# A feed-forward's second product as seven block products in place of eight, with its layer norm on another engine

## The chip, the cores and the metric

The kernel runs on one core of a Trainium2 chip. A core has five engines that run at the same time and wait for each other through semaphores: TensorE (PE in the profile; its weight loads, PEld, overlap with its matmuls), VectorE (DVE), ScalarE (ACT), GpSimd (POOL) and SyncE (SP), which here only issues DMA transfers. SBUF is the on-chip memory, PSUM the accumulator memory that TensorE writes. The metric is the device time of one execution in microseconds (us).

## The reference

A block over 4096 tokens of width 256, all in float32. `xn` is the normalized input; the output is the input plus an attention branch and a mixture of eight experts, both fed with `xn`.

```
xn   = layernorm(x)                                   # 4096 x 256
x1   = xn + attention(xn)                             # 8 heads, windows of 64
x2   = (x1 - mean) * rsqrt(var + eps) * gamma + beta  # second layer norm
h    = gelu(x2 @ W1 + b1)                             # 4096 x 1024
ffn  = x2 + h @ W2 + b2                               # second product: 1024 -> 256
moe  = sum over each token's two best experts of share * expert(xn)
out  = x + ffn + moe
```

## The kernel before

The order of the instructions on every engine is written out by hand: what the source says first comes first in that engine's queue. The work has three parts. A first stage (to about 50 us) normalizes the input, chooses experts and sorts tokens by expert. A long stage (to about 859 us) runs attention and the experts side by side; an expert's unit covers one or two tiles of 128 tokens, and its results go to the table `done` in device memory, the attention's to `x1d`. The last units (`whole`, lines 919 and 1301 to 1309) run only where the counts ask for them; those of one tile use matmuls with 128 moving columns (line 832). While this stage ends, at lines 1218 to 1235, the pools of attention are closed, `W1`, `W2` and the vectors are loaded, and the first group of the last stage is loaded and normalized.

The last stage is the feed-forward, from 859 us to the end: eight groups of 512 tokens (`NG`, four tiles `TG` of 128 tokens each). For a group `g`:

- `second_loads` (line 1070) loads `x2` from `x1d` and `acc` from the input, through SyncE's queue.
- `second_norm` (line 1077) normalizes: four `tensor_scalar` and the product with gamma on VectorE, then beta, `b2` and the sum into `acc` on GpSimd.
- `turned2` (line 1094) transposes `x2` on TensorE into `pt`, and VectorE copies it to `x2T`.
- `hidden` (line 1105) makes the eight chunks `ph` of 128x512 with two matmuls each; ScalarE writes gelu of them to `hT` (tile `hf`).
- `picked` (line 1120) gathers two rows of `done` per token with indirect DMAs that GpSimd issues, into eight buffers `got`; `combined` (line 1135) adds them to `acc` with their shares on VectorE.
- `second` (line 1143) makes the second product `pd`, 32 matmuls of 128x128 weights (`hT`) against 256 columns of `W2`, and VectorE adds it to `acc`; `store` writes `acc` out.

PSUM has seven banks that `bank` hands out in turn; a bank is written again only when its reader is done. In the loop TensorE's order is hidden(g), turned2(g+1), second(g-1), so the second product runs one group behind:

```
        if g > 0:
            acc = x2s.pop(g - 1)[0]
            list(second(g - 1, acc, before))
            combined(g - 1, acc, ys)
            store(g - 1, 0, TG, acc)
        before = hT
        ys = picked(g)
```

Of the kernel before, what the change touches and what calls it, by code (L numbers as in the profile page):

```python
# [32 lines left out]
F32 = mybir.dt.float32  # L33
# [68 lines left out]
def block_kernel(ctx: ExitStack, tc: tile.TileContext, a: dict, out: bass.AP):  # L102
# [11 lines left out]
    small = pool(ctx, "small", bufs=3)  # L114
    wexp = pool(ctx, "wexp", bufs=2)
    dram = ctx.enter_context(tc.tile_pool(name="dram", bufs=1, space=bass.MemoryType.DRAM))
# [12 lines left out]
    def halves(pb):  # L129
        return pb.rearrange("p (t n) -> p t n", t=2)  # L130
# [659 lines left out]

    he = pool(ctx, "he", bufs=2)
    sp = pool(att, "sp", right, bufs=2)
# [283 lines left out]

    def second_norm(g, acc, x2):

        for t in range(TG):
            i = g * TG + t  # L1080
            nc.vector.tensor_scalar(
                x2[:, t, :],
                x2[:, t, :],
                mv2[:, i, 0:1],
                r2[:, i : i + 1],
                ALU.subtract,
                ALU.mult,
            )
        nc.vector.tensor_tensor(x2, x2, bcast(gamma, TG, 1), ALU.mult)  # L1089
        nc.gpsimd.tensor_tensor(x2, x2, bcast(beta, TG, 1), ALU.add)  # L1090
        nc.gpsimd.tensor_tensor(acc, acc, bcast(b2, TG, 1), ALU.add)
        nc.gpsimd.tensor_tensor(acc, acc, x2, ALU.add)

    def turned2(g, x2):
        x2T = hf.tile([P, DC, G], F32, tag="x2T", name=f"x2T{g}")
        for c in range(DC):
            pt = bank(f"pt2_{g}_{c}")
            for t in range(TG):
                nc.tensor.transpose(  # L1099
                    pt[:, t * P : (t + 1) * P], x2[:, t, c * P : (c + 1) * P], ident  # L1100
                )
            nc.vector.tensor_copy(x2T[:, c, :], pt)  # L1102
        return x2T

    def hidden(g, x2T):
        hT = hf.tile([P, FC1, G], F32, tag="hf", name=f"hf{g}")
        for f in range(FC1):
            ph = bank(f"ph{g}_{f}")
            for c in range(DC):
                nc.tensor.matmul(  # L1110
                    ph,
                    W1[:, c, f * P : (f + 1) * P],
                    x2T[:, c, :],
                    start=(c == 0),
                    stop=(c == DC - 1),
                )
            nc.scalar.activation(hT[:, f, :], ph, AF.Gelu, bias=b1[:, f : f + 1])  # L1117
        return hT

    def picked(g):  # L1120
# [21 lines left out]

    def second(g, acc, hT):
        for t in range(0, TG, 2):
            pd = halves(bank(f"pd{g}_{t}"))
            for u in range(2):
                for f in range(FC1):
                    nc.tensor.matmul(  # L1148
                        pd[:, u, :],
                        hT[:, f, (t + u) * P : (t + u + 1) * P],  # L1150
                        W2[:, f, :],
                        start=(f == 0),
                        stop=(f == FC1 - 1),
                    )
            nc.vector.tensor_tensor(acc[:, t : t + 2, :], pd, acc[:, t : t + 2, :], ALU.add)  # L1155
            yield t

# [12 lines left out]
    STEPS = NT  # L1170
    flags = {}

    def load_unit(b):
# [5 lines left out]
    for b in range(ALWAYS):  # L1179
# [38 lines left out]
        if b == STEPS:  # L1218
            att.close()
            wf = pool(ctx, "wf", right)  # L1220
            hf = pool(ctx, "hf", right, bufs=2)
            accp = pool(ctx, "accp", right, bufs=4)
            got = pool(ctx, "got", right, bufs=8)
# [4 lines left out]
            late = pool(ctx, "late", right)  # L1228
            other.update({n: late for n in range(ALWAYS, BLOCKS, 3)})
            load_unit(ALWAYS)  # L1230
            for n in range(ALWAYS, BLOCKS):
                xs[n] = gather(n)
        if b == STEPS + 1:
            *_, r2 = rstd_of(mv2, root_of(mv2, NT, "b"), NT, "b")
            x2s[0] = second_loads(0)
        if 0 < b < STEPS:
# [55 lines left out]

    second_norm(0, *x2s[0])

# [123 lines left out]
```

## Time and profile before

| what | value |
|---|---|
| time, median of 3 runs | 1093.62 us (1093.41 to 1093.94) |
| profiled execution, its own time | 1094.16 us |
| its span in the profile | 1092.4 us |
| TensorE busy | 1079.8 us, 99% |
| VectorE, ScalarE, GpSimd busy | 598.3, 500.7, 503.3 us |
| granted TensorE clock | 1.00 throughout |
| last stage, TensorE's first transpose to the end | 858.8 to 1092.4 us |

The span is what the profiler saw on the core; the execution's own time has 1.76 us around it. A group of instructions is shown with its source line, engine, operation, the tile written and the tiles read, shapes and count; then busy time in us and the mean of one in ns; then idle time of the engine just before it and what ended that. The chain is the run of work that ended last, followed back from the end: start, duration, engine, tile, line, count. A float32 matmul leaves two records on TensorE (a transpose leaves one).

### The profile page before, as it was taken

What the parts mean: (1) busy time and instruction counts of PE and PEld (TensorE: products, weight loads), DVE (VectorE), ACT (ScalarE), POOL (GpSimd) and SP (SyncE); (2) the same over time, 40 slices, a digit from 0 to 9 for tenths busy, and PEclk for the clock granted to TensorE, in tenths of its full rate; (3) what the DMA queues carried; (4) which work ended last, traced back from release to release, by engine and by line L of the source; (5) the groups of instructions that cost most, each with busy time, mean ns of one, the idle gap of its engine ahead of it and who ended that gap; (6) DMA issues with size and microseconds to landing.
All of it is one profiled execution on the core that took longest, in us unless ns stands there. A gap on an engine that the chain in (4) does not pass through costs nothing. (4 is left out here: it accounts for less than half of the span.)

```text
span 1092.4 us, 18151 instructions
## 1 busy us (share of the span) xinstructions
PE 1079.8 (99%) x6424; PEld 855.0 (78%) x6424; DVE 598.3 (55%) x1633; ACT 500.7 (46%) x1170; POOL 503.3 (46%) x620
## 2 busy tenths in 40 slices
PE   8999999999999999999999999999999999999998
PEld 6577887887887888888888888888888666666667
DVE  6655766667666666676666666666542233332213
ACT  4526456645555556556645564566243322222220
POOL 5425543455346444653554455535123275555422
PEclk9999999999999999999999999999999999999999
DMA  9152445445355354454544544544386323333112
GB/s 293 62 232 78 141 148 175 172 140 176 134 167 178 127 182 161 159 181 148 194 140 158 168 177 141 197 149 177 134 311 221 104 77 97 96 97 97 58 58 77
DMA packets 60748, 163.37 MB, mean 150 GB/s; under 512 B 6288, under 2 KB 46608, under 8 KB 51184
## 3 DMA queue, kind: packets, MB, share of 16 engines
q1 hardware_dynamic: 54176, 144.48, 37.9%
q0 software_dynamic: 6480, 17.70, 5.8%
q8 instruction: 52, 0.85, 0.3%
q14 instruction: 40, 0.33, 0.1%
HBM read 140.28 MB, written 21.89 MB: 148 GB/s over the span
## 5 line engine op out<-in xcount | busy, mean ns | idle before, releaser
L832 PE MATMUL gu<-xsT,wg 128*128 128x256 f32 (+1 forms) x1632 | 362.5, 369 | 0.7 <-ACT xsT L824 0.7
L832 PEld LDWEIGHTS gu<-xsT,wg 128*128 128x128 f32 x1632 | 289.1, 190 | 45.3 <-DVE nm L961 8.6
L840 ACT ACTIVATE gs<-gu,wg 128x256 f32<-128x256 f32 (+1 forms) x204 | 93.0, 456 | 255.3 <-PE gu L832 249.3
L988 POOL TENSOR_TENSOR pr<-pr 128x256 f32<-128x256 f32 x128 | 93.1, 727 | 249.9 <-ACT pr L976 249.9
L841 DVE SCALAR_TENSOR_TENSOR hT<-gu,wg,gs 128x256 f32<-128x256 f32 (+1 forms) x204 | 95.2, 468 | 176.6 <-ACT gs L840 172.8
L894 PE MATMUL pe<-wd,hT 128*128 128x256 f32 x768 | 171.6, 379 | 0.0
L894 PEld LDWEIGHTS pe<-wd,hT 128*128 128x128 f32 x768 | 145.4, 190 | 20.5 <-issue 1.0
L989 POOL TENSOR_TENSOR pr<-pr,ident 128x256 f32<-128x256 f32 x128 | 126.3, 987 | 10.0
L976 ACT ACTIVATE pr<-pr,nm 128x256 f32<-128x256 f32 x256 | 127.4, 501 | 0.4
L1117 ACT ACTIVATE hf<-ph,b 128x512 f32<-128x512 f32 x64 | 44.1, 689 | 158.1 <-PE ph L1110 152.0
L1110 PE MATMUL ph<-x2T,W 128*128 128x512 f32 x256 | 111.3, 593 | 0.9 <-DVE x2T L1102 0.9
L1148 PE MATMUL pd<-W,hf 128*128 128x256 f32 x512 | 111.7, 379 | 0.0
L1148 PEld LDWEIGHTS pd<-W,hf 128*128 128x128 f32 x512 | 96.8, 190 | 13.3 <-issue 0.5
L961 DVE CUSTOM_DVE_ANT_0 pr<-ps,mask 128x256 f32<-128x256 f32 x256 | 90.7, 421 | 24.3 <-PE ps L947 24.3
L806 POOL DMA_INDIRECT xs<-xnd,token x71 | 68.9, 971 | 70.7 <-DVE paired_tiles L773 31.0
L1126 POOL DMA_INDIRECT got<-done,slot x64 | 63.4, 991 | 73.9 <-DVE acc L1139 60.9
L873 ACT ACTIVATE hT<-hT 128x512 f32<-128x512 f32 (+3 forms) x148 | 81.1, 548 | 32.0 <-DVE hT L841 21.8
L1110 PEld LDWEIGHTS ph<-x2T,W 128*128 128x128 f32 x256 | 48.5, 190 | 59.0 <-issue 57.6
L1090 POOL TENSOR_TENSOR x<-x,beta 128x1024 f32<-128x1024 f32 x8 | 18.8, 2349 | 88.4 <-DVE x L1089 88.4
L1155 DVE TENSOR_TENSOR acc<-pd,acc 128x512 f32<-128x512 f32 x16 | 11.0, 691 | 83.3 <-PE pd L1148 83.3
L1008 DVE TENSOR_TENSOR pr<-pr,rec 128x1024 f32<-128x1024 f32 x32 | 39.2, 1226 | 27.3 <-POOL pr L988 27.3
L976 ACT ACT_TABLE_LOAD x31 | 39.8, 1283 | 23.3 <-DVE nm L961 23.2
(213 smaller groups left out, 1440.5 us busy)
## 6 DMA issues: line engine op xcount, KB each, us to landing
wg<-in_gate_up SPq DMA_DIRECT2D x37, 1670.5 KB
wd<-in_down SPq DMA_DIRECT2D x37, 1024.0 KB
done<-y SPq DMA_DIRECT2D x30, 256.0 KB
x<-in_x SPq DMA_DIRECT2D x8, 512.0 KB
xnd<-xn SPq DMA_DIRECT2D x8, 512.0 KB
res<-xnd SPq DMA_DIRECT2D x16, 256.0 KB
x1d<-res SPq DMA_DIRECT2D x16, 256.0 KB
x<-x1d SPq DMA_DIRECT2D x8, 512.0 KB
```

What stands on the lines that cost most here:

```text
L806: nc.gpsimd.indirect_dma_start(out=x[:, t, :], out_offset=None, in_=xnd, in_offset=bass.IndirectOffsetOnAxis(ap=token[:, i : i + 1], axis=0),)
L832: nc.tensor.matmul(pb[:, k, :], w[:, lo : lo + P], xT[:, c, :], start=(c == 0), stop=(c == DC - 1),)
L840: nc.scalar.activation(gs, pb[:, 0, :], AF.Identity, bias=w[:, gb : gb + 1])
L841: nc.vector.scalar_tensor_tensor(hT[:, f, :], pb[:, 1, :], w[:, ub : ub + 1], gs, ALU.add, ALU.mult)
L873: nc.scalar.activation(hT[on, lo:hi, :], hT[on, lo:hi, :], AF.Silu)
L894: nc.tensor.matmul(pd, hT[:, f, t * P : (t + 1) * P], w[:, f * D : (f + 1) * D], start=False, stop=(f == FCM - 1),)
L961: nc.vector.tensor_tensor_reduce(out=pr[:, hh, j, :], in0=ps[hh][:, j, :], in1=mask[:, kind + j, :], scale=-1.0, scalar=-LOWEST, op0=ALU.a ...
L976: nc.scalar.activation(pr[:, hh, j, :], pr[:, hh, j, :], AF.Exp, bias=nm[:, j, hh : hh + 1], scale=-1.0, accum_out=sums[:, j, hh : hh + 1],)
L988: nc.gpsimd.tensor_tensor(first, first, second, ALU.add)
L989: nc.gpsimd.tensor_tensor(second, second, bcast(ident, 2, 1), ALU.mult)
L1110: nc.tensor.matmul(ph, W1[:, c, f * P : (f + 1) * P], x2T[:, c, :], start=(c == 0), stop=(c == DC - 1),)
L1148: nc.tensor.matmul(pd[:, u, :], hT[:, f, (t + u) * P : (t + u + 1) * P], W2[:, f, :], start=(f == 0), stop=(f == FC1 - 1),)
```

## The change

The second product of a group, (512 x 1024) times (1024 x 256), is seen as two by two blocks: tokens 0 to 255 and 256 to 511, hidden units 0 to 511 and 512 to 1023, output columns 0 to 127 and 128 to 255. Eight block products would make it; a scheme of Strassen's kind (Winograd's form) makes it with seven, from sums of blocks. The four sums of blocks of `W2` (tile `V2`) are made once on GpSimd, the four of a group's hidden activations (tile `hv`) on VectorE for each group, and the seven results are added to the four blocks of the output on VectorE, some by way of a tile `u`.

With it: the normalization goes to ScalarE as one activation per tile with scale and shift; gamma and beta are applied by the activation that takes the transposes out of PSUM, now on ScalarE too; `second_base` adds beta + b2 and gamma times the normalized rows to `acc` on VectorE; GpSimd keeps the gathers. In the loop, `second_loads` of group g+2 stands ahead of hidden(g), and `combined(g-1)` ahead of second(g-1). The pools of the experts close before the last stage, and its tiles `x2T`, `hf`, `hv`, `u` and `got` are placed where the experts' were.

```diff
-    def second_norm(g, acc, x2):
+    def second_norm(g, x2):
...
-            nc.vector.tensor_scalar(
+            nc.scalar.activation(
                 x2[:, t, :],
                 x2[:, t, :],
-                mv2[:, i, 0:1],
-                r2[:, i : i + 1],
-                ALU.subtract,
-                ALU.mult,
-            )
-        nc.vector.tensor_tensor(x2, x2, bcast(gamma, TG, 1), ALU.mult)
-        nc.gpsimd.tensor_tensor(x2, x2, bcast(beta, TG, 1), ALU.add)
-        nc.gpsimd.tensor_tensor(acc, acc, bcast(b2, TG, 1), ALU.add)
-        nc.gpsimd.tensor_tensor(acc, acc, x2, ALU.add)
+                AF.Identity,
+                bias=shift2[:, i : i + 1],
+                scale=r2[:, i : i + 1],
+            )
+
+    def second_base(g, acc, x2):
+
+        scaled = accp.tile([P, TG, D], F32, tag="scaled", name=f"scaled{g}", bufs=1)
+        nc.vector.tensor_tensor(acc, acc, bcast(beta_b2, TG, 1), ALU.add)
+        nc.vector.tensor_tensor(scaled, x2, bcast(gamma, TG, 1), ALU.mult)
+        nc.vector.tensor_tensor(acc, acc, scaled, ALU.add)
...
-            nc.vector.tensor_copy(x2T[:, c, :], pt)
+            nc.scalar.activation(
+                x2T[:, c, :], pt, AF.Identity, bias=beta_c[:, c : c + 1], scale=gamma_c[:, c : c + 1]
+            )
...
+    FH = FC1 // 2
+    F_LO, F_HI = slice(0, FH), slice(FH, FC1)
+    C1, C2 = slice(0, P), slice(P, D)
+
+    def sums_of_weights():
+        b11, b12, b21, b22 = W2[:, F_LO, C1], W2[:, F_LO, C2], W2[:, F_HI, C1], W2[:, F_HI, C2]
+        t1, t2, t3, t4 = (V2[:, k] for k in range(4))
+        for out_, left_, right_ in ((t1, b12, b11), (t2, b22, t1), (t3, b22, b12), (t4, b21, t2)):
+            nc.gpsimd.tensor_tensor(out_, left_, right_, ALU.subtract)
+
+    def sums_of_hidden(g, hT):
+        v = hf.tile([P, 4, FH, B], F32, tag="hv", name=f"hv{g}")
+        a11, a12, a21, a22 = hT[:, F_LO, 0:B], hT[:, F_HI, 0:B], hT[:, F_LO, B:], hT[:, F_HI, B:]
+        s1, s2, s3, s4 = (v[:, k] for k in range(4))
+        nc.vector.tensor_tensor(s1, a21, a22, ALU.add)
+        nc.vector.tensor_tensor(s2, s1, a11, ALU.subtract)
+        yield v
+        nc.vector.tensor_tensor(s3, a11, a21, ALU.subtract)
+        nc.vector.tensor_tensor(s4, a12, s2, ALU.subtract)
+        yield
+        return v
...
-    def second(g, acc, hT):
-        for t in range(0, TG, 2):
-            pd = halves(bank(f"pd{g}_{t}"))
...
-            nc.vector.tensor_tensor(acc[:, t : t + 2, :], pd, acc[:, t : t + 2, :], ALU.add)
+    def second(g, acc, hT, v):
+
+        t1, t2 = slice(0, 2), slice(2, 4)
+        u = hf.tile([P, 2, P], F32, tag="u", name=f"u{g}")
+
+        def product(n, left, right):
+            pb = bank(f"s{g}_{n}").rearrange("p (t n) -> p t n", n=P)[:, 0:2]
+            for t in range(2):
+                for f in range(FH):
+                    nc.tensor.matmul(
+                        pb[:, t, :],
+                        left[:, f, t * P : (t + 1) * P],
+                        right[:, f, :],
...
+        def add(t, cols, pb):
+            nc.vector.tensor_tensor(acc[:, t, cols], pb, acc[:, t, cols], ALU.add)
+
+        p1 = product(1, hT[:, F_LO, 0:B], W2[:, F_LO, C1])
+        nc.scalar.copy(u, p1)
+        add(t1, C1, u)
+        yield
+        p2 = product(2, hT[:, F_HI, 0:B], W2[:, F_HI, C1])
+        add(t1, C1, p2)
+        yield
+        p6 = product(6, v[:, 1], V2[:, 1])
+        nc.vector.tensor_tensor(u, p6, u, ALU.add)
+        add(t1, C2, u)
+        yield
+        p5 = product(5, v[:, 0], V2[:, 0])
+        add(t1, C2, p5)
+        add(t2, C2, p5)
+        yield
+        p7 = product(7, v[:, 2], V2[:, 2])
+        nc.vector.tensor_tensor(u, p7, u, ALU.add)
+        add(t2, C1, u)
+        add(t2, C2, u)
+        yield
+        p3 = product(3, v[:, 3], W2[:, F_HI, C2])
+        add(t1, C2, p3)
+        yield
+        p4 = product(4, hT[:, F_HI, B:], V2[:, 3])
+        add(t2, C1, p4)
+        yield
...
+            V2 = wf.tile([P, 4, FC1 // 2, P], F32, tag="V2", name="V2")
...
+            gamma_c, beta_c = column("gamma_c", DC, wf), column("beta_c", DC, wf)
...
         if b == STEPS + 1:
+            sums_of_weights()
...
-    second_norm(0, *x2s[0])
+    second_norm(0, x2s[0][1])
...
+    late_done.close()
+    experts_done.close()
+    hf = pool(ctx, "hf", right, bufs=2)
+    got = pool(ctx, "got", right, bufs=8)
     x2T = turned2(0, x2s[0][1])
-    second_norm(1, *x2s[1])
-    before = None
+    second_norm(1, x2s[1][1])
+    second_base(0, *x2s[0])
...
     for g in range(NG):
+        if g + 2 < NG:
+            x2s[g + 2] = second_loads(g + 2)
         hT = hidden(g, x2T)
+        if g + 1 < NG:
+            second_base(g + 1, *x2s[g + 1])
+        if g > 0:
+            acc = x2s.pop(g - 1)[0]
+            combined(g - 1, acc, ys)
         if g + 1 < NG:
             x2T = turned2(g + 1, x2s[g + 1][1])
         if g + 2 < NG:
-            x2s[g + 2] = second_loads(g + 2)
-            second_norm(g + 2, *x2s[g + 2])
+            second_norm(g + 2, x2s[g + 2][1])
+        ys = picked(g)
+        outs = second(g - 1, acc, *last) if g > 0 else iter(())
+        some(outs, 2)
+        sums = sums_of_hidden(g, hT)
+        last = hT, next(sums)
+        some(outs, 2)
+        some(sums, 1)
+        some(outs, 3)
         if g > 0:
-            acc = x2s.pop(g - 1)[0]
-            list(second(g - 1, acc, before))
-            combined(g - 1, acc, ys)
             store(g - 1, 0, TG, acc)
-        before = hT
-        ys = picked(g)
     acc = x2s.pop(NG - 1)[0]
     combined(NG - 1, acc, ys)
-    for t in second(NG - 1, acc, before):
-        store(NG - 1, t, 2, acc)
+    outs = second(NG - 1, acc, *last)
+    some(outs, 6)
+    store(NG - 1, 0, 2, acc)
+    some(outs, 1)
+    store(NG - 1, 2, 2, acc)
```

(`some(steps, n)` takes the next n steps of a generator, so the sums of the hidden activations stand between the additions of the products on VectorE.)

More of the change, by code (lines that the diff above doesn't have):

```diff
@@ L114, in block_kernel @@
     small = pool(ctx, "small", bufs=3)
-    wexp = pool(ctx, "wexp", bufs=2)
+    experts_done = ctx.enter_context(ExitStack())
+    wexp = pool(experts_done, "wexp", bufs=2)
     dram = ctx.enter_context(tc.tile_pool(name="dram", bufs=1, space=bass.MemoryType.DRAM))
@@ L788, in block_kernel @@
         nc.vector.tensor_tensor(share, share, bcast(tot, 2, 1), ALU.mult)
-    he = pool(ctx, "he", bufs=2)
+    he = pool(experts_done, "he", bufs=2)
     sp = pool(att, "sp", right, bufs=2)
@@ L1141, in combined @@
             )
-    def second(g, acc, hT):
-        for t in range(0, TG, 2):
-            pd = halves(bank(f"pd{g}_{t}"))
-            for u in range(2):
-                for f in range(FC1):
+    def second(g, acc, hT, v):
[5 more added lines that the diff above has]
+                for f in range(FH):
                     nc.tensor.matmul(
-                        pd[:, u, :],
-                        hT[:, f, (t + u) * P : (t + u + 1) * P],
-                        W2[:, f, :],
+                        pb[:, t, :],
+                        left[:, f, t * P : (t + 1) * P],
+                        right[:, f, :],
                         start=(f == 0),
-                        stop=(f == FC1 - 1),
+                        stop=(f == FH - 1),
                     )
-            nc.vector.tensor_tensor(acc[:, t : t + 2, :], pd, acc[:, t : t + 2, :], ALU.add)
-            yield t
+            return pb
+        def add(t, cols, pb):
[26 more added lines that the diff above has]
+        yield
     def store(g, t, n, acc):
@@ L1171, in block_kernel @@
     flags = {}
+    late_done = ctx.enter_context(ExitStack())
     def load_unit(b):
@@ L1220, in block_kernel @@
             wf = pool(ctx, "wf", right)
-            hf = pool(ctx, "hf", right, bufs=2)
             accp = pool(ctx, "accp", right, bufs=4)
-            got = pool(ctx, "got", right, bufs=8)
+            V2 = wf.tile([P, 4, FC1 // 2, P], F32, tag="V2", name="V2")
             W1, W2 = matrix(wf, "W1", F1, DC), matrix(wf, "W2", D, FC1)
@@ L1226, in block_kernel @@
             gamma, beta, b2 = (row(n, D, wf) for n in ("gamma", "beta", "b2"))
-            late = pool(ctx, "late", right)
+            gamma_c, beta_c = column("gamma_c", DC, wf), column("beta_c", DC, wf)
+            beta_b2 = wf.tile([P, D], F32, tag="beta_b2", name="beta_b2")
+            shift2 = wf.tile([P, NT], F32, tag="shift2", name="shift2")
+            late = pool(late_done, "late", right)
             other.update({n: late for n in range(ALWAYS, BLOCKS, 3)})
@@ L1233, in block_kernel @@
         if b == STEPS + 1:
+            sums_of_weights()
             *_, r2 = rstd_of(mv2, root_of(mv2, NT, "b"), NT, "b")
+            nc.vector.scalar_tensor_tensor(shift2, mv2[:, :, 0], -1.0, r2, ALU.mult, ALU.mult)
+            nc.vector.tensor_tensor(beta_b2, beta, b2, ALU.add)
             x2s[0] = second_loads(0)
@@ L1310, in block_kernel, with some @@
     x2s[1] = second_loads(1)
+    late_done.close()
+    experts_done.close()
+    hf = pool(ctx, "hf", right, bufs=2)
+    got = pool(ctx, "got", right, bufs=8)
     x2T = turned2(0, x2s[0][1])
-    second_norm(1, *x2s[1])
-    before = None
+    second_norm(1, x2s[1][1])
+    second_base(0, *x2s[0])
+    last = None
+    def some(steps, n):
+        for _ in range(n):
+            next(steps, None)
     for g in range(NG):
+        if g + 2 < NG:
+            x2s[g + 2] = second_loads(g + 2)
         hT = hidden(g, x2T)
+        if g + 1 < NG:
[3 more added lines that the diff above has]
+            combined(g - 1, acc, ys)
         if g + 1 < NG:
@@ L1397 @@
         "beta": v["beta"],
+        "gamma_c": chunks(v["gamma"], D),
+        "beta_c": chunks(v["beta"], D),
         "b1": chunks(v["b1"], F1),
```

## The prediction

> **What bounds the kernel now.** I read the page's busy shares first, then the chain that ended last in order of time, then the groups of instructions of the last 290 us with shapes kept apart, then the waits of TensorE and the last microseconds.
>
> ```profile
> PE 1079.8 (99%) x6424; PEld 855.0 (78%) x6424; DVE 598.3 (55%) x1633; ACT 500.7 (46%) x1170; POOL 503.3 (46%) x620
> ...
> 850.55 5.36 PE whole L832 x48
> ...
> 961.04 13.73 PE ph L1110 x32
> 974.77 0.87 PE pt L1099 x8
> 975.64 13.82 PE pd L1148 x64
> 989.46 13.73 PE ph L1110 x32
> ...
> PE ph L1110 <- DVE x2T L1102: 0.9, 2, 0.4
> ```
>
> TensorE is busy for 99% of the span. In the feed-forward, the stage that the change touches, the chain is one unbroken run of TensorE: hidden product `ph`, transposes `pt`, second product `pd`, each beginning where the one before ends, 13.73 + 0.87 + 13.82 = 28.42 us a group. The last line is the only wait of TensorE from 859 us to the end: 0.9 us, at the first two groups, for the copy of `x2T`. So a microsecond off the second product is a microsecond off the run, as long as TensorE doesn't begin to wait.
>
> ```profile
> L1148 PE MATMUL pd<-W,hf 128*128 128x256 f32 x512 | 111.7, 379 | 0.0
> L1148 PEld LDWEIGHTS pd<-W,hf 128*128 128x128 f32 x512 | 96.8, 190 | 13.3 <-issue 0.5
> L832 PE MATMUL whole<-xsT,wg 128*128 128x128 f32 x96 | 11.0, 275 | 0.0
> L1117 ACT ACTIVATE hf<-ph,b 128x512 f32<-128x512 f32 x64 | 44.1, 689 | 158.1 <-PE ph L1110 152.0 <-issue 6.2
> L1139 DVE SCALAR_TENSOR_TENSOR acc<-got,share,acc 128x256 f32<-128x256 f32 x64 | 29.0, 482 | 6.8 <-DMA got<-done,slot 5.4 <-issue 0.3
> L904 DVE TENSOR_TENSOR y<-pe,wd 128x256 f32<-128x256 f32 x4 | 1.7, 425 | 5.9 <-PE pe L894 5.9
> L1089 DVE TENSOR_TENSOR x<-x,gamma 128x1024 f32<-128x1024 f32 x8 | 9.8, 1225 | 0.3
> ...
> 932.62:961.04 28.42, 28.42 (x105) 19.07 (x105) 8.71 (x17) 5.51 (x8) 14.95 (x11) 1.00 0.31 93
> ...
> 1087.31 0.48 DVE L1139 SCALAR_TENSOR_TENSOR acc<-got,share,acc 128x256 f32<-128x256 f32 x1 [0.90 <-DMA got<-done,slot]
> 1087.71 1.28 DVE L1155 TENSOR_TENSOR acc<-pd,acc 128x512 f32<-128x512 f32 x2
> ```
>
> Here the reader sees the prices, then the busy time of each engine in one group (TensorE, its weight loads, VectorE, ScalarE, GpSimd, then granted clock and DMA). A float32 matmul leaves two records, so 64 records are 32 matmuls. Records are pipelined: the mean of one (379 ns) is its latency, and its cost is the busy time over the count. The last two lines are the tail: TensorE ends at 1085.78 + 1.89 = 1087.67 us, and two additions of 128x512, the last held back by the late gathers, end at 1088.99.
>
> **The second product (the gain).** It goes out as 32 matmuls with 256 moving columns, 64 records at 13.82 / 64 = 215.9 ns. In come seven products of 8 matmuls with 128 moving columns: 56 matmuls, 112 records. The question is what a record costs at half the columns. The nearest row is line 832 in the `whole` units: the same 128x128 float32 weights, a new set in every matmul, 128 columns, two records each. The chain gives 5.36 us for 48 of them, 111.7 ns. So 112 x 111.7 = 12.51 us against 13.82: 1.31 us less a group and 10.5 us in eight. The floor is half of 215.9, 107.9 ns: 12.09 us, 13.8 us in eight. I take the row.
>
> A rule speaks against this. The Trainium skill, "TensorE: Matmul & The Clock Gate", section "Back-to-back issue gap", says that in a stream of weight load and matmul both set the spacing, and gives about 81 ns at 128 columns and 131 ns at 512: time falls much more slowly than columns. A straight line puts 256 columns at 98 ns, so halving would leave 81 / 98 = 0.83 of the time of a record: 0.83 x 215.9 = 179 ns, 112 of them 20.0 us, an estimate of 6.2 us MORE a group, 50 us in eight. By the rows of this trace halving leaves 111.7 / 215.9 = 0.517. The rows are float32 in this kernel at a granted clock of 1.00; they decide, and the rule becomes the slower rival.
>
> **The additions around it (VectorE).** A group kept VectorE busy for 8.71 us (the fourth figure of the stretch of one group, above: 2 additions of 128x512, 4 normalizations and the product with gamma, 2 copies of `x2T`, 8 weighted additions). It will have 11 of 128x256 for the seven products (0.425 by line 904: 4.7), 4 sums of the hidden activations of 128x1024 (1.225 by line 1089: 4.9), 3 for the base (3.7) and the same 8 weighted ones (0.482: 3.9): 17.1 us in a period of 13.73 + 0.87 + 12.51 = 27.1.
>
> **The order in a group.** Let T be the end of the last `ph`. ScalarE is a queue: the last gelu ends at T + 0.7, the two copies of `x2T` with gamma and beta (0.69 each, line 1117's shape) at T + 2.1, the four normalizations of the group after next at T + 4.6 (0.61 each, the row of line 464), and only then the copy `u` of the first product (0.46, line 840), at T + 5.0. What is queued behind these is that copy, and VectorE's whole sequence waits for it. TensorE ends its products at T + 2.7, 4.4, 6.2, 8.0, 9.8, 11.6 and 13.4. VectorE follows: two additions to T + 5.9, two sums to 8.3, the additions of products 6 and 5 to 10.0, two sums to 12.5, product 7 to 13.8, product 3 to 14.2, product 4 to 14.6; the base of another group to 18.3 and the weighted additions to 22.2. It then waits until T + 27.1 + 5.0, so it has 10 us to spare a group. TensorE waits for none of it: PSUM has seven banks in turn, the bank of product 7 is wanted by the fifth `ph` at T + 13.4 + 6.9 = T + 20.3 and is free at T + 12.9; that of product 4, by the seventh `ph` at T + 23.7, free at T + 14.6. The sums are used one group later. So VectorE's added 8 us and ScalarE's added 4.3 us cost nothing; were the 10 us of cover gone, each further microsecond would be one of the group.
>
> **GpSimd and the DMA queue.** Out go three operations of 128x1024 a group (2.35 each); the eight gathers (about 1 us) stay. They wait for the weighted additions that free their buffers. These used to stand behind the second product's additions and now stand before them, so the gathers start some 20 us earlier in their group and the weighted additions never wait. Once, four subtractions on half of W2 (0.73 us at 256 columns, 2.35 at 1024: about 1.2 each, 5 us) go on GpSimd at about 805 us, where it stood idle for 18 us. SyncE gets two small loads at 794 us (about 0.5 each to issue); behind them stands the load of the next unit's second weights, issued at 795.5 and used at 816, and it can spare 1 us. The loads of the group after next move ahead of the hidden product; SyncE's queue has the store of group g-2 before them, which waits until T + 14.6; `x2` then lands by T + 20 (5 us for the pair at 859.9) and is wanted at T + 29. Nothing.
>
> **The start of the stage.** The normalization of group 1 now stands on ScalarE ahead of the gelus of group 0 and waits for its load, which landed at 864.96. Behind it stand a table load (1.28) and all gelus: the first would end near 864.96 + 2.4 + 1.3 + 0.7 = 869.4. TensorE wants that bank back for the eighth `ph`, at 860.25 + 7 x 1.72 = 872.3. It has 3 us of cover; a landing 5 us later would stop TensorE for 2 us, once. By the order of the built program identity and gelu share one table: a single load stands in the stage. The backlog pushes the copy of `x2T` for group 1 by about 0.1 us. The pools that close early put the hidden tiles where experts' tiles were; by the built program's waits the first `x2T` needs only transfers done by then. Cost 0.1.
>
> **The tail.** Before, 1088.99 - 1087.67 = 1.32 us of additions stood between TensorE's end and the last store. After, one addition of 128x256 (0.43 and 0.04 to start): 0.85 us less.
>
> **The sum**, against the profiled execution of 1094.16 us (span 1092.4 and 1.76 around it): 1094.16 - 10.5 - 0.85 + 0.1 = 1082.9. The median of the runs, 1093.62, lies 0.54 below that execution, so 1082.4.
>
> **The rivals.**
> - *Weight loads bind (slower).* The 190 ns of a weight load are latency that must be served one by one at 112 a group: 112 x 190 = 21.3 us, 7.5 more a group, 60 in eight: 1153; by the skill's ratio 1142. The row of 190 ns speaks for it; line 832, with as many loads at 111.7 ns, against it. It decides from 13.82 / 112 = 123.4 ns a record.
> - *VectorE's sequence sets the pace (smaller gain).* Small additions with strides (2x128 out of 256 columns) or the copy `u` behind a full ScalarE queue might cost more than their rows. VectorE's 17.1 us would have to become more than 27.1 to be felt; with 28 us a group (1.6 times each price) the gain is 0.4 x 8 + 0.85 = 4 us: 1089 to 1090. No row shows such prices.
> - *One stall at the start.* The load of group 1 lands late beside the gathers that now start there: 2 to 5 us once: 1085 to 1087. Two fewer loads in flight than before (those of group 2 now wait for VectorE) speak against it.
> - *The floor.* Records at 107.9 to 109 ns (the transposes: 0.87 / 8 = 109): 12.09 to 12.2 us a group: 1079 to 1080.
>
> **How the numbers follow.** As summed, with prices within a few per cent: 0.74, its own range 1080.5 to 1084.5. The floor 0.06, the start 0.07, VectorE's pace 0.06, weight loads 0.06, and 0.01 that it all cancels. The range that leaves out no more than 2 in 10 is 1078.5 to 1086.5: it takes in the floor and the start. Differences under 0.2% (2.2 us) can't be told from none here. Faster: 0.93; same 0.01; slower 0.06.
>
> **What would show it.** Right: the seven-product row with 896 records at about 100 us busy (111.7 each); the chain as an unbroken run of 13.7, 0.87 and 12.5 us; VectorE about 17 us in each 27 and waiting for TensorE or ScalarE; gathers done before they are wanted; at the end one addition of 0.43 after TensorE. Wrong: TensorE idle before `ph` or a product with VectorE or ScalarE named, records above 120 ns, a gap at 872 us, table loads between gelus.

## The result, and the profile after

The changed kernel took 1083.73 us (median of 4 runs, 1082.85 to 1085.82) against 1093.78 us of the kernel before (4 runs, 1093.41 to 1096.14): a ratio of 0.9906, 95% interval 0.9886 to 0.9927. Two later series of the same kernel gave 0.9911 (0.9895 to 0.9928) and 0.9899 (0.9883 to 0.9916). It is faster by about 10 us, and its time is 1.3 us above the 1082.4 that was predicted.

Some executions of either kernel are 1 to 3 us longer than the others, and in the profiled ones of the changed kernel this is lost before the last stage is reached (last section), so below it is the *stage* that is compared: from the start of the first `ph` to the end of the span in each profiled execution. Before, that is 1092.4 - 860.25 = 232.15 us; after, 1084.0 - 862.96 = 221.04. The stage became 11.11 us shorter; the sum of the prediction for it was 10.5 + 0.85 - 0.1 = 11.25. (Spans are given to 0.1 us, so stages are known to about that.)

The start of the stage before, then, for the changed kernel, the page's first line, TensorE's only wait in the stage, and the chain that ended last (start, duration, engine, tile, line, count):

```profile
860.25 13.97 PE ph L1110 x32
```

```profile
PE 1071.3 (99%) x6808; PEld 858.0 (79%) x6808; DVE 656.5 (61%) x1707; ACT 527.0 (49%) x1226; POOL 452.7 (42%) x600
```

```profile
PE ph L1115 <- ACT x2T L1105: 1.1, 2, 0.6
```

```profile
862.96 14.01 PE ph L1115 x32
...
960.02 13.73 PE ph L1115 x32
973.76 0.87 PE pt L1102 x8
974.63 12.51 PE s L1186 x112
987.14 13.73 PE ph L1115 x32
...
1055.10 25.02 PE s L1186 x224
...
1080.15 0.42 DVE acc L1196
```

TensorE is still busy for 99% of the span. The chain is still one unbroken run; only the middle term of a group has changed, from 13.82 to 12.51 us, and a group from 28.42 to 13.73 + 0.87 + 12.51 = 27.11. At the end stands one addition of 0.42 us. TensorE's only waits are the two for the first copies of `x2T`, 1.1 us where they were 0.9.

The groups of the stage, with shapes kept apart (busy us, mean ns of one, idle before):

```profile
L1186 PE MATMUL s<-V,hv 128*128 128x128 f32 x384 | 44.2, 275 | 0.0
L1186 PE MATMUL s<-W,hf 128*128 128x128 f32 x256 | 29.9, 275 | 0.0
L1186 PE MATMUL s<-W,hv 128*128 128x128 f32 x128 | 15.6, 275 | 0.0
L1186 PE MATMUL s<-V,hf 128*128 128x128 f32 x128 | 15.6, 275 | 0.0
L1146 DVE TENSOR_TENSOR hv<-hf 128x1024 f32<-128x1024 f32 x8 | 9.7, 1217 | 5.2 <-ACT hf L1122 5.2
```

The seven products are the four rows of line 1186, 896 records in all; a record costs 12.51 / 112 = 111.7 ns by the chain. (The busy times of the rows overlap a little where one product follows another, so the price is read from the chain.) The sums of hidden activations cost 1.22 us each on VectorE. One group as a stretch (busy of TensorE, its weight loads, VectorE, ScalarE, GpSimd; granted clock; DMA share and GB/s), and VectorE and ScalarE inside it (start, duration, in brackets the idle time before):

```profile
932.90:960.02 27.12, 27.12 (x154) 19.42 (x153) 15.87 (x26) 9.04 (x15) 7.93 (x8) 1.00 0.32 98
```

```profile
950.55 0.36 ACT L1199 COPY u<-s 128x256 f32<-128x256 f32 x1
950.94 0.43 DVE L1196 TENSOR_TENSOR acc<-u,acc 128x256 f32<-128x256 f32 x1 [10.38 <-ACT u L1199]
...
960.06 0.42 DVE L1196 TENSOR_TENSOR acc<-s,acc 128x256 f32<-128x256 f32 x1 [0.38 <-PE s L1186]
...
963.93 3.75 DVE L1173 SCALAR_TENSOR_TENSOR acc<-got,share,acc 128x256 f32<-128x256 f32 x8
```

VectorE went from 8.71 to 15.87 us in a group, ScalarE from 5.51 to 9.04, GpSimd fell from 14.95 to 7.93. The 10.38 us in brackets are VectorE's longest idle time in a group, ended by the copy `u`: this is the cover that is left after all the added work. How much more would fit under it is one of the things that the experiments ask.

### The profile page after: what moved, and what is told of

Same layout as the page of the kernel before. It is cut to its first block, busy times and chain, and to the rows that moved or that the text cites. A ratio compares the mean times of both kernels' runs of the same rounds, so it can differ in the third digit from the quotient of the medians.

```text
span 1084.0 us, 19063 instructions
## 1 busy us (share of the span) xinstructions
PE 1071.3 (99%) x6808; PEld 858.0 (79%) x6808; DVE 656.5 (61%) x1707; ACT 527.0 (49%) x1226; POOL 452.7 (42%) x600
## 5 line engine op out<-in xcount | busy, mean ns | idle before, releaser
L1196 DVE TENSOR_TENSOR acc<-u,acc 128x256 f32<-128x256 f32 x32 | 12.9, 423 | 70.1 <-ACT u L1199 69.6
L1010 DVE TENSOR_REDUCE same<-pr 128x8 f32<-128x1024 f32 x32 | 39.1, 1222 | 19.8 <-POOL pr L990 19.8
L977 ACT ACTIVATION_READ_ACCUMULATOR pr<-pr,nm 128x1 f32 x256 | 48.4, 189 | 0.0
L1186 PE MATMUL s<-V,hv 128*128 128x128 f32 x384 | 44.2, 275 | 0.0
```

Of the source, the lines that this page charges most:

```text
L977: nc.scalar.activation(pr[:, hh, j, :], pr[:, hh, j, :], AF.Exp, bias=nm[:, j, hh : hh + 1], scale=-1.0, accum_out=sums[:, j, hh : hh + 1],)
L1186: nc.tensor.matmul(pb[:, t, :], left[:, f, t * P : (t + 1) * P], right[:, f, :], start=(f == 0), stop=(f == FH - 1),)
```

## The experiments

All stages at a glance; the differences are to the stage of the changed kernel.

| kernel | stage, us | difference | time, median (range), us | ratio to before |
|---|---|---|---|---|
| before | 232.15 | +11.1 | 1093.78 (1093.41 to 1096.14) | |
| changed | 221.04 | | 1083.73 (1082.85 to 1085.82) | 0.9906 |
| again | 221.02 | 0.0 | 1084.74 (1084.08 to 1085.21) | 0.9911 |
| again2 | 221.02 | 0.0 | 1083.33 (1083.00 to 1084.31) | 0.9899 |
| eight | 231.47 | +10.4 | 1093.60 (1092.93 to 1096.56) | 0.9996 (0.9987 to 1.0005) |
| seven_only | 226.05 | +5.0 | 1087.70 (1087.30 to 1089.79) | 0.9945 (0.9928 to 0.9963) |
| late | 226.55 | +5.5 | 1090.82 (1089.99 to 1093.73) | 0.9966 (0.9958 to 0.9974) |
| oldnorm | 233.46 | +12.4 | 1095.79 (1094.99 to 1097.88) | 1.0018 (1.0010 to 1.0025) |
| gathers_first | 221.06 | 0.0 | 1086.44 (1085.31 to 1087.29) | 0.9921 (0.9904 to 0.9937) |
| all_vector | 221.76 | +0.7 | 1087.99 (1086.53 to 1088.08) | 0.9935 (0.9918 to 0.9951) |
| pool3 | 228.32 | +7.3 | 1094.33 (1091.63 to 1095.80) | 0.9996 (0.9986 to 1.0006) |
| dve6 | 221.66 | +0.6 | 1085.85 (1085.23 to 1087.26) | 0.9922 (0.9906 to 0.9939) |
| dve14 | 276.26 | +55.2 | 1140.50 (1140.04 to 1140.96) | 1.0423 (1.0403 to 1.0444) |
| split64 | 321.01 | +100.0 | 1185.77 (1185.52 to 1186.02) | 1.0836 (1.0815 to 1.0858) |

**The same kernel again**, once with each of two sets.

> The changed kernel as it is, to narrow the ratio and to see whether the short half clock at 10 to 17 us, which its profiled run shows and that of before doesn't, belongs to it. Theory (the gain is TensorE's seven products and the tail, the clock drop is chance): 10.5 to 11.5 us below before, ratio 0.9895 to 0.9905, and a granted clock of 1.00 in most runs. Rival (the change brings the clock drop): 8 to 9 us below before, ratio 0.992, with the drop in nearly every run.

> The changed kernel once more, beside the last case on one chip: a stage of 221.0 us, and 9 to 11 us below before.

The stage is 221.02 us both times, the same as the first within its 0.1. A stage can thus be compared to well under a microsecond, where the whole time can't. The whole time met only the second expectation: the first series came out 9.3 us below before, between the two theories, and its profiled execution has the lower clock at the start again; the second came out 10.6 below. What can be said of the clock stands in the last section.

**Eight products in the new order.** Everything else of the change stays: the norm on ScalarE, the order of the loop, the pools. Only the second product is as it was, and the sums are left out.

```diff
     def second(g, acc, hT, v):
...
+        for t in range(0, TG, 2):
+            pd = halves(bank(f"pd{g}_{t}"))
+            for u in range(2):
+                for f in range(FC1):
                     nc.tensor.matmul(
+                        pd[:, u, :],
+                        hT[:, f, (t + u) * P : (t + u + 1) * P],
+                        W2[:, f, :],
...
-            sums_of_weights()
```

> Everything of the change stays (norm on ScalarE, base on VectorE, loads, gathers and weighted additions moved ahead), but the second product is again 32 matmuls of 256 columns and its sums are left out. Theory: a group takes 28.4 us again, the tail ends with one addition of 128x512 (0.69): 10.5 us above the changed kernel, 0 to 1 us below the kernel before. Rival (part of the gain is due to the moved engines or the moved order): clearly below before, by 3 us or more.

The stage is 231.47 us, 0.68 below before and 10.43 above the changed kernel. The chain of this kernel:

```profile
961.31 13.73 PE ph L1115 x32
975.04 0.87 PE pt L1102 x8
975.92 13.82 PE pd L1182 x64
...
1087.97 0.69 DVE acc L1189
```

With the new order and the new engines the group is 28.42 us as it was. So in the run of groups the change of engines and of order is worth nothing by itself, 0.7 us at the tail, and the products are worth 10.4, about 8 x (13.82 - 12.51) = 10.5.

**Where 111.7 ns comes from.** The prediction took this price from a row and could not say what set it. Each matmul is cut into two of 64 columns with the same weights loaded for each: twice the weight loads and matmuls, the same columns in all.

```diff
             for t in range(2):
-                for f in range(FH):
...
+                for h in range(2):
+                    n64 = slice(h * P // 2, (h + 1) * P // 2)
+                    for f in range(FH):
+                        nc.tensor.matmul(
+                            pb[:, t, n64],
+                            left[:, f, t * P : (t + 1) * P],
+                            right[:, f, n64],
```

> Each product's matmuls are cut into two of 64 moving columns, so there are 224 records and 224 weight loads a group for the same columns. If spacing goes by columns plus some 5 ns (111.7 at 128): about 58 ns a record, 13.1 us a group, 4 to 5 us in all above the changed kernel. If a weight load of 128 columns sets a floor near what 128 columns take (107 to 112 ns): about 24.5 us a group, 96 us above the changed kernel; then 128 columns is where weight loads begin to bind.

The stage is longer by 99.97 us. The end of this kernel's chain:

```profile
1130.38 49.98 PE s L1188 x448
```

That is 49.98 / 448 = 111.6 ns a record at 64 columns, as at 128, and 8 x 112 x 111.6 ns = 100.0 us, the whole difference. Half the columns cost the same, so these records have a floor of 111.6 ns that doesn't depend on their columns; 256 columns cost 215.9 ns, so 128 lie just at that floor. A second halving of the blocks, down to 64 columns, would take 49 products of two matmuls, 196 records: 21.9 us a group at this price, an estimate, in place of 12.51. What sets the floor stays open. Each of these records comes with a weight load of 128x128 float32, which may be it; no run changes the load alone. It isn't a floor of every record: the attention's `po`, with weights of 128x32 and 128 columns, come every 28 ns (24 of them from 779.06 to 779.74 in the changed kernel), but they differ in more than the load, since each fills only a quarter of the output's partitions.

**How much cover VectorE has.** Behind `combined(g-1)` stand n products of gamma and beta into a tile that nothing reads, 6 in one kernel and 14 in the other.

```diff
+    def more_work(g, n):
+        spare = accp.tile([P, TG, D], F32, tag="spare", name=f"spare{g}", bufs=1)
+        for _ in range(n):
+            nc.vector.tensor_tensor(spare, bcast(gamma, TG, 1), bcast(beta, TG, 1), ALU.mult)
...
             combined(g - 1, acc, ys)
+        more_work(g, 6)
```

> The changed kernel with six more VectorE products of 128x1024 in each group (7.35 us), behind the weighted additions and ahead of the additions of the products, written to a tile that nobody reads. Theory (10 us of cover a group): within 0.5 us of the changed kernel, TensorE without a new wait. Rival (VectorE's sequence is nearly the pace, or its work slows its neighbours): 3 us or more above it.

> The same with fourteen products (17.2 us a group), 7 us over the cover. Theory: VectorE becomes the bound at about 34 us a group; with the first groups still covered and the lag paid at the end, 40 to 55 us above the changed kernel. Were the cover twice as large as worked out, nothing to 5 us; were there none, 130 us.

One of them costs 1.225 us. TensorE's waits in the stage, first the new one with 6, then the two longest with 14 (total, times, longest):

```profile
PE s L1191 <- issue: 0.4, 1, 0.4
```

```profile
PE ph L1120 <- ACT hf L1127: 28.2, 32, 3.8
PE s L1191 <- issue: 5.0, 8, 0.8
```

Six are 7.3 us a group and cost 0.6 in the whole stage, all of it in the first second product (13.09 us in place of 12.51): TensorE stops there once, in the middle of one of the seven products, with nothing named that it waits for. It is a stop of the kind described in the last section and no sign of a missing cover; after it nothing is lost. Fourteen are 17.2 us a group; less the 10.4 idle ones of the timeline that is 6.8 too many, 54 us in eight groups, and 55.2 were measured, just above the range expected. The cover is 10 us, as predicted, and when it is gone each further microsecond is one of the group.

**The order of the weighted additions.** They and the gathers go back behind the second product's additions.

```diff
-        if g > 0:
-            acc = x2s.pop(g - 1)[0]
-            combined(g - 1, acc, ys)
...
-        ys = picked(g)
...
         if g > 0:
+            combined(g - 1, acc, ys)
             store(g - 1, 0, TG, acc)
+        ys = picked(g)
```

> The changed kernel with the weighted additions and the gathers back behind the second product's additions, as before the change. Theory: nothing in the run of groups, but at the end the last gathers start 14 us after the last hidden product and land at 28, and the eleven additions of the last seven products queue behind the last weighted addition: VectorE ends near T + 33 in place of T + 25.5, so 6 to 8 us above the changed kernel. Rival (the order is worth only what the tail of before showed): 1 us.

The stage is longer by 5.5 us, a little under what was expected. Its chain leaves TensorE at the end:

```profile
1053.89 12.52 PE s L1186 x112
...
1076.73 2.79 DMA got<-done,slot
...
1079.61 0.48 DVE acc L1173
...
1084.07 0.33 DVE acc L1196
```

The run of groups isn't touched: from the first `ph` to the start of the last two second products it is 1053.89 - 861.75 = 192.14 us, as in the changed kernel. By its price TensorE's last product would end at about 1078.9 us (1053.89 + 2 x 12.52); two stops like that of dve6 put it off to 1080.15. The last gather lands at 1079.5, and behind the last weighted addition VectorE still has the additions of seven products to make, and these reach to 1084.4. With eight products two additions stood there; with seven, the old order costs 5.5 us.

**Seven products in the old order.** The products and sums go into the kernel before; its loop and its norm on VectorE and GpSimd stay.

```diff
     for g in range(NG):
...
-            list(second(g - 1, acc, before))
+        outs = second(g - 1, acc, *last) if g > 0 else iter(())
+        some(outs, 2)
+        sums = sums_of_hidden(g, hT)
+        last = hT, next(sums)
...
+        if g > 0:
             combined(g - 1, acc, ys)
             store(g - 1, 0, TG, acc)
```

> Seven products and their sums alone, in the old order: norm on VectorE and GpSimd, copy of the transposes on VectorE, loads behind the hidden product, weighted additions and gathers behind the second product. Theory (from the runs so far: the products are worth 10.4 us in the stage; contention with GpSimd is covered in the run of groups when it isn't part of a loop; the old order costs 5 to 6 us at the tail): the stage from the first hidden product to the end 5 to 7 us longer than the changed kernel's 221.0, so 226 to 228, and the time 4 to 6 us below before. Rival (GpSimd's norm lengthens VectorE's sums so far that TensorE waits in every group): 232 or more, no gain left.

The stage is 226.05 us, as expected: 6.1 below before, 5.0 above the changed kernel. The waits of TensorE and the row of one of the sums:

```profile
PE ph L1111 <- DVE x2T L1103: 0.8, 2, 0.4
```

```profile
L1143 DVE TENSOR_TENSOR hv<-hv,hf 128x1024 f32<-128x1024 f32 x8 | 20.0, 2501 | 0.3
```

By the timeline TensorE is done at 1077.04, 217.0 us after its first `ph` at 860.05, against 227.4 before: the whole gain of the products is there. What is lost is the tail: 9.1 us from TensorE's end to the end of the span where before had 4.7 and the changed kernel 3.9. And one of the four sums takes 2.50 us on the average where it takes 1.22 in the changed kernel: with the norm on GpSimd something slows VectorE, here inside the cover.

**The old norm in the new order.** The norm is again four `tensor_scalar` and a product on VectorE and three operations on GpSimd, the copy of `x2T` is on VectorE; products and loop stay as changed.

```diff
-            nc.scalar.activation(
+            nc.vector.tensor_scalar(
...
+        nc.vector.tensor_tensor(x2, x2, bcast(gamma, TG, 1), ALU.mult)
+        nc.gpsimd.tensor_tensor(x2, x2, bcast(beta, TG, 1), ALU.add)
+        nc.gpsimd.tensor_tensor(acc, acc, bcast(b2, TG, 1), ALU.add)
+        nc.gpsimd.tensor_tensor(acc, acc, x2, ALU.add)
...
+            nc.vector.tensor_copy(x2T[:, c, :], pt)
```

> Seven products stay; the norm goes back to VectorE with beta, b2 and the sum on GpSimd, and the copy of the transposes to VectorE. Theory: VectorE has 10 us to spare in a group either way and GpSimd 10, so TensorE never waits: within 1 us of the changed kernel. Rival (without ScalarE's help VectorE or GpSimd sets the pace): 3 us or more above it, with TensorE waiting in every group.

It was expected within 1 us, and came out 12.4 us longer: more than the whole gain. The chain of this kernel is no longer one of TensorE:

```profile
957.76 1.28 DVE x2T L1103 x2
959.04 1.30 DVE x L1082 x4
...
960.36 1.24 DVE x L1090
...
961.74 2.40 POOL x L1091
964.13 3.31 POOL acc L1092
...
967.51 3.22 POOL acc L1093
...
970.88 0.97 POOL got L1156
...
980.47 4.84 DMA got<-done,slot
...
985.80 1.28 DVE x2T L1103 x2
```

It is a loop of 985.80 - 957.76 = 28.0 us, through two queues that are served in order, against 27.1 for a group of TensorE. On VectorE the copy of `x2T` stands behind the weighted additions, these wait for gathers, the gathers stand on GpSimd behind the three operations of a norm, that norm waits for VectorE's half, and VectorE's half stands behind the copy. TensorE then waits for what VectorE does late, first 3.1 us for a copy of `x2T` and 3.1 for an addition that frees a bank, then some 0.6 in each group:

```profile
PE ph L1111 <- DVE u L1202: 3.1, 1, 3.1
PE s L1182 <- DVE x2T L1103: 3.1, 1, 3.1
PE ph L1111 <- DVE u L1210: 2.5, 5, 0.6
```

Most of the loss, 8.7 us, has come by the fourth group: its `ph` starts 78.67 us after the first, where it is 69.94 in the changed kernel. From there on it is about 1 us a group, as 28.0 against 27.1 says.

Two explanations were left: the loop through GpSimd's queue, or simply the work of the norm on VectorE and GpSimd, which also take longer here beside each other. Three kernels tell them apart.

**Gathers ahead of the norm.** The kernel just shown, with one step exchanged in GpSimd's queue.

```diff
         if g + 2 < NG:
+            ys_next = picked(g)
             second_norm(g + 2, *x2s[g + 2])
-        ys = picked(g)
+        else:
+            ys_next = picked(g)
+        ys = ys_next
```

> The kernel of the last case (seven products, norm back on VectorE and GpSimd), with one more edit: GpSimd issues a group's gathers before its three operations of the norm, not after. Theory A (that kernel lost its gain to a loop: weighted additions wait for gathers, gathers stand behind GpSimd's norm, that waits for VectorE's norm, which stands behind the copy of the transposes and the weighted additions): the loop is cut, and it comes within 1.5 us of the changed kernel. Theory B (GpSimd's elementwise work and VectorE's slow each other so far that VectorE sets the pace): still 5 us or more above the changed kernel.

The stage is 221.06 us, that of the changed kernel. TensorE waits 0.8 us for the first two copies and for nothing else that the trace names, although one sum still takes nearly twice its price:

```profile
L1142 DVE TENSOR_TENSOR hv<-hf 128x1024 f32<-128x1024 f32 x8 | 18.0, 2246 | 0.0
```

So the 12.4 us were the loop. How far the stretched operations lengthen it is not separated: its three GpSimd operations take 8.9 us, and at the 2.35 each of the kernel before they would take 7.05 and leave a loop of about 26.2 us, an estimate, shorter than a group. The same norm on the same engines costs nothing once GpSimd issues the gathers first: VectorE is then busy for 22.5 of 27.1 us (the stretch 934.00 to 961.12), and the stretched operations lie inside the cover.

**Everything on VectorE.** The changed kernel with norm and copy on VectorE; GpSimd keeps the gathers only.

```diff
-            nc.scalar.activation(
+            nc.vector.tensor_scalar(
                 x2[:, t, :],
                 x2[:, t, :],
...
-            nc.scalar.activation(
...
+            nc.vector.tensor_scalar(
+                x2T[:, c, :], pt, gamma_c[:, c : c + 1], beta_c[:, c : c + 1], ALU.mult, ALU.add
```

> The changed kernel with the norm and the copy of the transposes (gamma and beta in it) on VectorE in place of ScalarE; GpSimd keeps the gathers only. VectorE has 1.4 + 1.3 us more a group, some 20 of 27. Theory (what matters is that GpSimd is out of the way, not that ScalarE does it): within 1 us of the changed kernel. Rival (VectorE needs ScalarE's help): 3 us or more above.

221.76 us, 0.7 more, all of it in the first second product (13.26 us in place of 12.51), where TensorE stops once in the middle of a product, as in dve6. ScalarE isn't needed for the gain; what matters is that the norm isn't in front of the gathers.

**GpSimd busy beside VectorE.** The changed kernel with three products of gamma and beta on GpSimd behind each group's gathers, into a tile that nothing reads.

```diff
+    def more_work(g):
+        spare = accp.tile([P, TG, D], F32, tag="spare", name=f"spare{g}", bufs=1)
+        for _ in range(3):
+            nc.gpsimd.tensor_tensor(spare, bcast(gamma, TG, 1), bcast(beta, TG, 1), ALU.mult)
...
         ys = picked(g)
+        more_work(g)
```

> The changed kernel with three GpSimd products of 128x1024 in each group behind its gathers, written to a tile that nobody reads: contention without a new order. If GpSimd's and VectorE's elementwise work contend: VectorE's operations that run beside them take up to 3 us in place of 1.2 and GpSimd's 3.3 in place of 2.35; the cover of 10 us a group takes that up, so within 1 us of the changed kernel in time. If they don't contend (the long ones had another cause): durations as without them.

Nobody waits for these products, and still the stage is 7.3 us longer, where at most 1 was expected. The timeline of one group (start, duration, engine, line):

```profile
956.91 9.12 POOL L1100 TENSOR_TENSOR spare<-gamma,beta 128x1024 f32<-128x1024 f32 x3
957.16 3.23 DVE L1151 TENSOR_TENSOR hv<-hf 128x1024 f32<-128x1024 f32 x1
960.42 3.32 DVE L1152 TENSOR_TENSOR hv<-hv,hf 128x1024 f32<-128x1024 f32 x1
963.66 0.41 DVE L1211 TENSOR_TENSOR u<-s,u 128x256 f32<-128x256 f32 x1
964.11 2.19 DVE L1201 TENSOR_TENSOR acc<-u,acc 128x256 f32<-128x256 f32 x1
```

While GpSimd runs, the two sums take 3.23 and 3.32 us in place of 1.22, and the addition of `u` 2.19 in place of 0.42; GpSimd's own products take 9.12 / 3 = 3.04 us. The addition in between, which reads a product from PSUM and `u` from SBUF, takes its usual 0.41. The time is another matter. TensorE stops in the second product:

```profile
1006.11 7.48 PE s L1191 x67
1013.60 0.78 issue
1014.37 5.18 PE s L1191 x45
```

Up to the last `ph` (1047.30 - 863.08 = 184.22 us against 1041.37 - 862.96 = 178.41) that makes 5.8 us, all of it inside six second products, which take 13.1 to 13.8 us in place of 12.51. But these stops are not shown to come from the stretched operations. A product is 16 records, so 67 records are four products and three records of the fifth: TensorE stops in the middle of a product whose bank it already holds, and the trace names nothing that it waits for. In this kernel's first second product 0.8 us are lost (13.32 us) while the sums beside it take their usual 1.22. And stops of this kind stand in dve6, dve14, late and all_vector too, where GpSimd has no added work (last section). Whether GpSimd's burst brings more of them stays open. The remaining 1.5 us are in the tail, and there the chain that ended last does run through the stretched sums: a burst meets additions that have no cover.

For the durations a rule of the Trainium skill bears on the measurement: "SBUF — State Buffer", section "SBUF: two separate sides", says that VectorE and GpSimd share a pair of ports under an exclusive lock, held for a whole instruction, and that VectorE needs it when it has two SBUF inputs, against a GpSimd operation that reads SBUF. The runs agree: of these VectorE operations those with two SBUF inputs are stretched, and those with a PSUM input are not. The lengths fit too: GpSimd's first product, by a narrower view, runs from 956.91 for 2.40 us, so the first sum, begun at 957.16, would wait 2.15 us and take 1.22 of its own, 3.37 in all by estimate; 3.23 were measured.

## Why the prediction was right

**The price of a record.** Right to the last digit: 111.7 ns from the 128-column row of the `whole` units, 12.51 us for a group's second product, and 10.4 us in the stage by the comparison with eight (10.43), where 10.5 was said. The floor of half a 256-column record (107.9 to 109 ns, the fourth rival) wasn't reached. The rule of the Trainium skill that was weighed there ("TensorE: Matmul & The Clock Gate", "Back-to-back issue gap") would have made it 20.0 us a group by the prediction's estimate. Its statement that weight load and matmul together set the spacing fits the floor that split64 shows, but no run separates the two. Its ratio of 0.83 for half the columns doesn't hold for these float32 records: 111.7 / 215.9 = 0.517. The rival that weight loads bind had the price wrong: it wanted 190 ns a record, and a record with a new load costs 111.7. That something binds at 111.6 ns, and that 128 columns arrive there just in time, the prediction didn't know: its own price came from a row at the same number of columns and so has the floor in it. For a split to 64 columns the same reasoning by columns would have missed by some 95 us (split64: 4 to 5 expected from it, 100 measured).

**VectorE and its cover.** Worked out: 17.1 us busy in a group and 10 idle. Measured: 15.9 busy, and 10.4 idle in front of the copy `u`. The order within the group was right too, with T = 946.64 the end of a last `ph`: `u` starts at T + 3.9 and ends at T + 4.3 (predicted T + 5.0: the copy takes 0.36 in place of 0.46, and the four normalizations 2.07 in place of 2.44), product 4 is added at T + 13.8 (14.6), the weighted additions end at T + 21.0 (22.2). The rival that VectorE's sequence sets the pace needed prices 1.6 times as high; dve6 and dve14 show where it would have begun: between 7.3 and 17.2 us more a group, and by the loss of dve14 at about 10.

**Start and tail.** From the first to the second `ph` it is 15.45 us after and 15.28 before: 0.17 where 0.1 was said. The feared stall at the eighth `ph` didn't come. Group 1's load landed 2.5 us later than before, and the normalization, one table load and the gelus followed:

```profile
867.43 2.08 ACT L1082 ACTIVATE x<-x,shift,r_b 128x256 f32<-128x256 f32 x4 [3.85 <-DMA x<-x1d]
869.53 1.28 ACT L1122 ACT_TABLE_LOAD   x1
```

so the first gelu, which begins at 870.82, ended at about 871.5. The whole stage was 2.7 us later than before, and the bank was wanted at 862.96 + 7 x 1.72 = 875.0, 3.5 us after that. From TensorE's end to the end of the span it is 1084.0 - 1080.13 = 3.87 us against 1092.4 - 1087.67 = 4.73: 0.86 less, predicted 0.85.

**The sum, and the 1.4 us that were missing.** The sum before rounding was 1082.37, and the median is 1083.73: 1.36 more. In the stage 11.11 us came of 11.25, 0.14 too few. The median of before moved from 1093.62 to 1093.78 with a fourth run, 0.16. The medians differ by 10.05, so the other 1.06 us lie outside the stage. In the profiled execution of the changed kernel it is 2.7 us that are lost there, nearly all in the first 50 us of the program, which the change doesn't touch (last section); the execution of the median time wasn't traced.

**What was right for less than the full reason.** "GpSimd and the DMA queue: nothing" held for the whole change, but not because these operations don't matter. The prediction costed the three operations that leave GpSimd, and the place of the weighted additions, one by one, as hidden work: nothing for the first, 0.85 for the tail. The runs show that the parts of the change lean on each other:

- Products alone, in the old order (seven_only): 6.1 us of stage.
- Order and engines alone, with eight products (eight): 0.7 us.
- Products and order, the norm left where it was (oldnorm): -1.3 us, slower than before.
- All of it: 11.1 us.

With seven products eleven additions follow where two did, and the weighted additions ahead of them are worth 5.0 to 5.5 us; the prediction counted only the length of the last addition. And once the weighted additions stand ahead, gathers behind a norm in GpSimd's queue close a loop of 28 us; the norm on ScalarE is one way to cut it, the gathers ahead of the norm another, equal one. Nothing in the sum would have told the reader that the norm could not stay where it stood: that the whole change had this part in it is to that extent luck for the prediction.

## What to carry to other kernels

Price a halved matmul by a row of the same kernel with that shape, number type and rate of weight loads, and look for the floor under it before planning a further split: here it is 111.6 ns a record with a new 128x128 float32 weight, reached just at 128 columns. Where VectorE or GpSimd has slack on the average, ask in which order its queue stands: the same work cost nothing or 12.4 us, by the place of the gathers in GpSimd's queue alone. Follow a wait round until it closes or ends, and do so for each part of a change left out, since parts that are worth nothing alone can be what another part needs.

## What the hardware showed that was not expected

- VectorE and GpSimd slow each other by much more than a few per cent: a sum of 128x1024 with both inputs in SBUF takes 2.8 to 3.3 us in place of 1.22 (pool3, oldnorm), an addition of 128x256 with both in SBUF 2.1 to 3.0 in place of 0.42, GpSimd's operation 3.0 to 3.3 in place of 2.35; operations with a PSUM input are not touched (0.41).
- In the profiled execution of the changed kernel the granted clock was 0.60 from 10 to 17 us after the start (0.50 of it from 12 to 17), where the profiled execution of before had 1.00; its first `ph` came 2.7 us later. In the two repetitions the clock from 12 to 17 us was 0.67 and 0.66 and the first `ph` 2.1 and 1.2 us later; in seven_only and eight it came as in before. By the mean clock of each execution it isn't this kernel's alone: of the 65 executions of before beside the experiments 17 have 0.997 or 0.998, and all of these took 1095.0 us or more; of the changed kernel's twelve 5 have 0.996 to 0.998. These counts are too small to say whether the change makes it more frequent. How busy TensorE was just before doesn't explain it either: from 10 to 12 us it was busy for 0.50 us in the changed kernel, but for 0.78 in pool3, which kept 1.00, and for 1.50 in dve6, which fell to 0.66.
- In six kernels (late, pool3, gathers_first, all_vector, dve6, dve14) TensorE lost another 1.6 to 2.7 us at 777 to 783 us after the start, in a stage that the edits of these six don't touch. Its records then come a few at a time, every 1.43 or 1.44 us, with no wait that the trace names; in late:

```profile
777.48 0.81 PE L833 MATMUL gu<-xsT,wg 128*128 128x256 f32 x3
778.92 1.09 PE L833 MATMUL gu<-xsT,wg 128*128 128x256 f32 x3 [0.63 <-issue]
780.35 0.59 PE L833 MATMUL gu<-xsT,wg 128*128 128x256 f32 x2 [0.34 <-issue]
```

  The stops inside second products have the same beat (in pool3 four records at 928.15, the next at 929.59), and among the kernels here only these six have them. It fits that their medians lie higher than their stages say (gathers_first: a stage as in the changed kernel, a median 2.7 us above it). These six ran on two chips, and every kernel of the other runs whose chip is on record ran on two others, so kernel and chip can't be told apart here. The cause wasn't found.
